# Self-attention's reciprocals two slots behind their maxima, half the transposes and all weighings a slot later, keys projected in other slots

## The chip, the cores and the metric

The kernel runs on one core of a Trainium2 chip. The metric is the device time of one execution in microseconds (us). Three runs of the kernel before took 1098.41, 1099.25 and 1100.58 us; the median is 1099.25. Times inside an execution come from one profiled execution, whose own time was 1095.93 us.

A core has five engines that run their own instruction queues in order: TensorE (PE in the profile; its weight loads are PEld), VectorE (DVE), ScalarE (ACT), GpSimd (POOL) and SyncE (SP), which here issues nearly all transfers. An instruction starts when it has reached the head of its queue and the semaphores that it waits for have come.

## The reference

One transformer block in float32, for 2 sequences of 1024 tokens with 256 features, and a context of 154 tokens with 192 features for each. There are 16 heads of 64, so the attention is 1024 wide. Cut to what matters:

```python
h = layernorm(x, ln1_g, ln1_b)
x = attention(h, h, sa_wq, sa_wk, sa_wv, sa_wo, sa_bo) + x      # self-attention, 1024 keys
h = layernorm(x, ln2_g, ln2_b)
x = attention(h, cond, ca_wq, ca_wk, ca_wv, ca_wo, ca_bo) + x   # cross-attention, 154 keys
h = layernorm(x, ln3_g, ln3_b)
p = h @ ff_w1 + ff_b1
out = (p[..., :1024] * gelu(p[..., 1024:])) @ ff_w2 + ff_b2 + x

def attention(xq, xkv, wq, wk, wv, wo, bo):      # per head, d = 64
    attn = softmax(q @ k.T * 64 ** -0.5)
    return (attn @ v) @ wo + bo
```

## The kernel before, in words

The program is one long sequence written out by hand: a loop over slots p = 0 to 127 for self-attention, one over slots c = 0 to 47 for cross-attention, then the feed-forward part. The order in which the Python code emits instructions is the order in each engine's queue.

**Units and slots.** Heads are taken in pairs; a pair of one sequence is a unit, and there are 16 units. A unit has two halves of 512 queries (index h), and a half has SH = 4 slots. So a unit has 8 slots, and a slot handles 128 queries of two heads, as two groups of 64. In what follows the slots of a half are called 0 to 3.

**A slot of self-attention** (`self_first`, line 642). TensorE makes the scores of the two groups, in two PSUM buffers `s`, 1024 columns each (line 489). Because of the packing of the array, one row of a score tile holds half of a query's 1024 keys for two heads; a query's other half lies 32 partitions away. VectorE takes the maxima of each score tile (line 650). ScalarE makes the exponents into tiles `p` with their sums (`exponents`, line 500; four instructions a slot). SP then sends maxima and sums to the partitions of the other half with four small transfers (`exchange`, line 510; `st<-st` in the profile). In the next slot, `join` (line 514) works out on POOL and ScalarE what the two halves need to share a denominator: differences `dd` (lines 518 and 519), factors `ee` (line 521), products `zz` (line 523) and denominators `den` (line 525). VectorE takes the reciprocal `rd` (line 596) and POOL scales the exponents in place with four instructions (line 600). A slot later still, VectorE transposes the two scaled tiles in blocks of 32 into `pT` (line 614). When the four slots of a half are transposed, TensorE weighs the values with them, in two parts of one slot each (`self_values`, line 618; matmuls at line 535), into two PSUM banks `po`, and ScalarE copies the result out (line 635).

**The order inside slot p before** (loop at line 1139): scores and both maxima of p; copies that the slot before left over; exponents of p; `join` of p-1; the exchange of p; both transposes of p-2 (LAG = 2); an output addition if one is due; the reciprocal and the four scalings of p-1; a bias addition on POOL or a moved transfer if one is due (`later`, in slots 2, 4 and 6 of a unit); weight loads; and last the slot's other work on TensorE. So on VectorE the queue is: maximum, maximum, transpose, transpose (both of p-2), addition, reciprocal (of p-1). On POOL it is: dd, dd, zz, den (of p-1), four scalings (of p-1), bias addition.

**The slot's other work** (lines 1160 to 1178). Slots 2 and 3 of a half weigh the half before. In the first half of a unit, slots 0 and 1 project the next unit's queries and keys (lines 358, 373, 381). In the second half, slot 0 projects the next unit's values (line 389; their second copy goes out by SP, lines 405 and 406), and slot 1 takes two output projections (line 463; VectorE adds them to x, line 470). Layer-norm steps for later use (`norm_beside`, line 322) run beside them: statistics on VectorE (lines 236 and 237), variance and power on POOL (lines 242 and 246), normalisation on ScalarE or POOL, transposition on TensorE (line 276).

**What cross-attention needs from earlier.** The context is transposed (`turn_context`, line 194). Its keys are projected for each of the eight pairs (`context_keys`, line 718; matmuls at line 722; weights by `load_keys`, line 712). Before, pairs 0 to 2 are projected in slot 13, pairs 3 and 4 in slot 125, and pairs 5 to 7 in cross-attention's slot 10. The values of the last 26 context tokens are projected in three pieces (`context_ends`, line 736, 192 columns in each of two halves; EC at line 42).

**Cross-attention** has three slots in a unit: scores, maxima (line 803), exponents (line 814), reciprocal (line 822), scaling (line 825), transposes (line 841), then eight transfers by SP that regroup the transposed tiles (`cross_regroup`, line 847; `wf<-pT_ca` in the profile), and the weighing that reads them (`cross_values`, line 861, `poc` at line 877).

**Buffers.** Tiles `p` come from the pool `pp`, 6 buffers, which at the start also holds the context tiles `cn` and the tile `rows` of layer-norm gains and biases until they are transposed. `pT` has two buffers (one for each of two halves), `s` two, `st8` and the other small tiles four.

Of the kernel before, what the change touches and what calls it, by code (L numbers as in the profile page):

```python
# [8 lines left out]
F32 = mybir.dt.float32  # L9
# [4 lines left out]
P = 128  # L14
# [4 lines left out]
def tile_transformer_block(ctx: ExitStack, tc: tile.TileContext, a: dict, out: bass.AP):  # L19
# [22 lines left out]
    EC = 3 * HR  # L42
# [21 lines left out]
    pp_ = ctx.enter_context(tc.tile_pool(name="pp", bufs=6))  # L64
# [121 lines left out]

    def turn_rows():
        pt = spare["bank"]("p_rows")
        nc.tensor.transpose(
            pt[:, :n_rows - n_cols], rows, ident[:n_rows - n_cols, :n_rows - n_cols]  # L190
        )
        return lambda: nc.scalar.copy(cols[:, n_cols:], pt[:, :n_rows - n_cols])
# [24 lines left out]
    def norm_pieces(kind, b, first=False):  # L217
# [31 lines left out]
        def normalize(t):  # L249
# [5 lines left out]
            pool, tag = (one, "xn") if narrow(kind, b) and not first else (pp_, "P")  # L255

            xn = pool.tile([P, nh, 2, D // nh], F32, tag=tag, name=f"xn_{ln}_{b}_{t}")
            st["xn", t] = xn
# [10 lines left out]
        def turn(t):  # L269
# [4 lines left out]
            for i in range(2 * D // P):  # L274
# [3 lines left out]
                    st["xn", t].rearrange("p c i d -> p (c i d)")[:, i * P:(i + 1) * P], ident)  # L278
# [235 lines left out]
    def join(u, st):  # L514
# [4 lines left out]
        nc.gpsimd.tensor_scalar(dd, dd, 0.0, 1.0, op0=ALU.min, op1=ALU.mult)  # L519
        ee = small.tile([P, 2, 4], F32, tag="ee", name=f"ee_{u}")  # L520
        nc.scalar.activation(ee, dd, AF.Exp)  # L521
        zz = small.tile([P, 2, 4], F32, tag="zz", name=f"zz_{u}")
# [3 lines left out]
        return ee, den  # L526
# [18 lines left out]
    drain = []  # L545
# [42 lines left out]
    joins, groups, halves = [], [], {}  # L588

    def scale_groups(u, st, members):  # L590

        ee, den = join(u, st)

        def reciprocals():
            rd = small.tile([P, 4], F32, tag="rd", name=f"rd_{u}")
            nc.vector.reciprocal(rd, den)  # L596
            for i, pr in enumerate(members):
                for j in range(2):
                    c = 2 * i + j
                    nc.gpsimd.tensor_scalar(  # L600
                        pr[:, j, :], pr[:, j, :], rd[:, c:c + 1], ee[:, 0, c:c + 1],
                        op0=ALU.mult, op1=ALU.mult,
                    )
                groups.append(pr)

        return reciprocals

    def turn_groups(p):
        h, g = divmod(p, SH)
        if g == 0:  # L610
            halves[h] = pt_.tile([P, 2 * NK, QH // 2], F32, tag="pT", name=f"pT_{h}")
        for i in range(2):
            c = (2 * g + i) * KB
            nc.vector.transpose(  # L614
                halves[h][:, :, c:c + KB], groups.pop(0).rearrange("p j (n k) -> p (j n) k", k=KB)
            )
# [25 lines left out]
    def self_first(p):  # L642
# [6 lines left out]
        for i in range(2):  # L649
            nc.vector.tensor_reduce(st[:, 0, 0, i, :], sc[i], AX.X, ALU.max, negate=True)  # L650

        def then():
            members = [exponents(f"{p}_{i}", sc[i], st, i) for i in range(2)]
            late = scale_groups(*joins.pop(0)) if joins else None
            exchange(st)
            joins.append((p, st, members))
            return late
# [25 lines left out]
    def load_ahead(p):  # L683
# [12 lines left out]
        if p == SH:  # L696
            load_keys(0, 3)
        if p == SA - SH - 6:
            load_keys(3, 2)
# [381 lines left out]
    with tc.manual_schedule():  # L1081
# [48 lines left out]
        take("k", 2)  # L1130
        ahead = load_ahead_parts()
        ahead[0] = lambda: load_weights("sa", units[1][1], "k")
        ahead[1] = lambda: load_weights("sa", units[1][1], "q")
        side.append((True, (), turn_rows))
        side.extend((True, (), lambda b=b: turn_context(b)) for b in range(B))
# [3 lines left out]
        for p in range(SA):  # L1139
# [7 lines left out]
            late = then()  # L1147
            if p >= LAG:
                turn_groups(p - LAG)
            if adds:  # L1150
                adds.pop(0)()
            if late:
                late()
# [7 lines left out]
            if h == 0 or hg < LAG:  # L1161

# [3 lines left out]
                ui, n = divmod(p, 2 * SH)  # L1166
                f = (ui - NPAIR // 2 - 1) * EC
                if n == 0 and 0 <= f < DA // 2:
# [167 lines left out]
```

## Time and profile before

| what | value |
|---|---|
| median of three runs | 1099.25 us |
| the profiled execution | 1095.93 us |
| its span, first to last instruction | 1094.1 us |
| self-attention's slots 0 to 127 | 17.9 to about 710 us |
| cross-attention, then feed-forward | to about 871 us, then to the end |

A line of a group in the profile gives the line of the code, the engine, the operation, what it writes and reads, shapes and count; then the busy time of the group and the mean duration of one in ns; then the idle time of the engine just before these instructions, and what ended most of it. A line of a wait names who waited for whom, with the total in us, the number of times and the longest. A line of the timeline gives the start, the duration, the engine, the line of the code, the operation and the number of instructions merged in it; in brackets stands the idle time before it and what ended it. SPq is SyncE's queue of transfers.

### The profile page before, as it was taken

What the parts mean: (1) busy time and instruction counts of PE and PEld (TensorE: products, weight loads), DVE (VectorE), ACT (ScalarE), POOL (GpSimd) and SP (SyncE); (2) the same over time, 40 slices, a digit from 0 to 9 for tenths busy, and PEclk for the clock granted to TensorE, in tenths of its full rate; (3) what the DMA queues carried; (4) which work ended last, traced back from release to release, by engine and by line L of the source; (5) the groups of instructions that cost most, each with busy time, mean ns of one, the idle gap of its engine ahead of it and who ended that gap; (6) DMA issues with size and microseconds to landing.
All of it is one profiled execution on the core that took longest, in us unless ns stands there. A gap on an engine that the chain in (4) does not pass through costs nothing.

```text
span 1094.1 us, 44913 instructions
## 1 busy us (share of the span) xinstructions
PE 1074.5 (98%) x18388; PEld 711.6 (65%) x18388; DVE 892.2 (82%) x1297; ACT 639.2 (58%) x2061; POOL 730.1 (67%) x1552
## 2 busy tenths in 40 slices
PE   8999999999999999999999999899999999999998
PEld 6555666556765565565555655466776677788887
DVE  5889899998989999999999999977877877655442
ACT  5666666667667666666766676565565554242221
POOL 2767777777777777777777777676756785475331
PEclk9999999999999999999999999999999999999999
DMA  3222112122111111111110111036775545000000
GB/s 83 65 59 52 47 44 55 34 51 53 27 40 44 29 43 33 38 42 24 42 42 15 42 30 32 18 82 163 171 172 119 117 108 120 1 10 15 11 15 29
DMA packets 104094, 60.71 MB, mean 55 GB/s; under 512 B 32330, under 2 KB 94674, under 8 KB 103890
## 3 DMA queue, kind: packets, MB, share of 16 engines
q1 hardware_dynamic: 102514, 57.07, 22.1%
q8 instruction: 145, 2.38, 0.9%
q10 hardware_dynamic: 1376, 0.79, 0.3%
q14 instruction: 59, 0.48, 0.1%
HBM read 27.91 MB, written 2.10 MB: 27 GB/s over the span
## 4 chain that ended last, share of the span: by engine, by line
PE 70%; DVE 7%; ACT 7%; DMA 5%; POOL 4%; SPq 3%; issue 3%; DVEq 0%; POOLq 0%; ACTq 0%
PE s L489 13%; PE po L535 12%; ACT p L500 6%; PE pf L1064 5%; PE py_ca L463 5%; PE py_sa L463 4%; DVE st L650 4%; PE pq_ca L358 4%; PE poc L877 4%; DMA st<-st 4%; PE pb L998 3%; PE pv_sa L389 3%; PE sc L798 3%; PE pk_sa L358 3%; SPq L510 3%
## 5 line engine op out<-in xcount | busy, mean ns | idle before, releaser
L500 ACT ACTIVATE p<-s,st 128x512 f32<-128x512 f32 x512 | 345.3, 687 | 196.1 <-DVE st L650 189.8
L600 POOL TENSOR_SCALAR p<-p,rd,ee 128x512 f32<-128x512 f32 x512 | 385.7, 768 | 48.0 <-DVE rd L596 47.0
L650 DVE TENSOR_REDUCE st<-s 128x2 f32<-128x1024 f32 x256 | 300.9, 1216 | 23.4 <-PE s L489 9.1
L614 DVE STREAM_TRANSPOSE pT<-p 128x1024 f32<-128x1024 f32 x256 | 302.3, 1218 | 0.3 <-POOL p L600 0.3
L489 PE MATMUL s<-k_sa,q_sa 64*32 64x512 f32 x4096 | 259.8, 592 | 8.3 <-ACT p L500 7.4
L535 PE MATMUL po<-pT,v_sa 64*32 64x256 f32 x8192 | 239.6, 376 | 0.7 <-DVE pT L614 0.7
L535 PEld LDWEIGHTS po<-pT,v_sa 64*32 64x32 f32 x8192 | 174.2, 106 | 74.8 <-issue 21.2
L489 PEld LDWEIGHTS s<-k_sa,q_sa 64*32 64x32 f32 x4096 | 81.5, 106 | 112.1 <-ACT p L500 56.3
L814 ACT ACTIVATE p<-sc,neg 128x154 f32<-128x154 f32 x256 | 96.4, 406 | 83.7 <-DVE rden L822 80.5
L825 POOL TENSOR_SCALAR p<-p,rden 128x154 f32<-128x154 f32 x256 | 96.8, 398 | 59.1 <-DVE rden L822 58.6
L500 ACT ACTIVATION_READ_ACCUMULATOR p<-s,st 128x1 f32 x512 | 103.9, 203 | 0.0
L523 POOL TENSOR_TENSOR zz<-ee,st 128x8 f32<-128x8 f32 x128 | 25.9, 202 | 74.9 <-ACT ee L521 74.9
L389 PEld LDWEIGHTS pv_sa<-sa_wv,hT_ln 64*128 64x128 f32 x1024 | 58.9, 188 | 14.3 <-issue 5.0
L389 PE MATMUL pv_sa<-sa_wv,hT_ln 64*128 64x128 f32 x1024 | 62.3, 275 | 0.0
L463 PE MATMUL py_ca<-ca_wo,o_ca 128*128 128x256 f32 x256 | 60.0, 382 | 0.5 <-DVE o_ca L891 0.5
L463 PE MATMUL py_sa<-sa_wo,o_sa 128*128 128x256 f32 x256 | 59.7, 385 | 0.0
L518 POOL TENSOR_TENSOR dd<-st 128x8 f32<-128x8 f32 x128 | 25.6, 200 | 50.2 <-DMA st<-st 45.6
L463 PEld LDWEIGHTS py_sa<-sa_wo,o_sa 128*128 128x128 f32 x256 | 47.3, 190 | 17.9 <-ACT v_sa L398 5.9
L358 PE MATMUL pq_sa<-hT_ln,sa_wq 64*32 64x512 f32 (+1 forms) x976 | 58.1, 587 | 0.0
L358 PE MATMUL pq_ca<-hT_ln,ca_wq 64*128 64x512 f32 (+1 forms) x304 | 58.0, 590 | 0.0
L358 PE MATMUL pk_sa<-hT_ln,sa_wk 64*32 64x512 f32 x960 | 57.1, 590 | 0.9 <-ACT q_sa L373 0.9
L803 DVE TENSOR_REDUCE neg<-sc 128x6 f32<-128x924 f32 (+1 forms) x48 | 47.9, 999 | 11.9 <-PE sc L798 11.8
(118 smaller groups left out, 1452.4 us busy)
## 6 DMA issues: line engine op xcount, KB each, us to landing
wf<-pT_ca SPq DMA_DIRECT2D x128, 128.0 KB, 2.4
st<-st SPq DMA_DIRECT2D x512, 1.0 KB, 1.8
v_sa<-v_sa SPq DMA_DIRECT2D x32, 256.0 KB, 3.8
sa_wq<-in_L_xattn_sa_wq_dram SPq DMA_DIRECT2D x32, 128.0 KB, 3.3
sa_wk<-in_L_xattn_sa_wk_dram SPq DMA_DIRECT2D x32, 128.0 KB, 3.0
sa_wv<-in_L_xattn_sa_wv_dram SPq DMA_DIRECT2D x32, 128.0 KB, 3.5
ca_wq<-in_L_xattn_ca_wq_dram SPq DMA_DIRECT2D x32, 128.0 KB, 4.2
wf<-in_L_xattn_ff_w_dram SPq DMA_DIRECT2D x12, 256.0 KB
```

What stands on the lines that cost most here:

```text
L358: nc.tensor.matmul(pq[r][f:f + m, at:at + n], lhsT=wt[own, c, f:f + m], rhs=h[own, c, t0:t0 + n], start=(c == 0), stop=(c == NH - 1), tile ...
L389: nc.tensor.matmul(pv[r][:, i * P:(i + 1) * P], lhsT=h[own, c, i * P:(i + 1) * P], rhs=wt[own, c, :], start=(c == 0), stop=(c == NH - 1), ...
L463: nc.tensor.matmul(py[:, e * D:(e + 1) * D], lhsT=o[:, i, (t + e) * P:(t + e + 1) * P], rhs=wo[kind][:, g * HP + i, :], start=(i == 0), st ...
L489: nc.tensor.matmul(sc[a4 * KB:(a4 + 1) * KB, j, :], lhsT=q[r, c:c + KB], rhs=k[r, h * HB:(h + 1) * HB], start=True, stop=True, tile_positi ...
L500: nc.scalar.activation(pr[:, j, :], sc[:, j, :], AF.Exp, bias=st[:, 0, 0, i, j:j + 1], accum_out=st[:, 0, 1, i, j:j + 1],)
L535: nc.tensor.matmul(po[a2][d:d + KB, :QH // 2], lhsT=v[r, t, e, d:d + KB], rhs=pT[r, d // DH * NK + n, :], start=(t == 0 and e == 0), stop= ...
L600: nc.gpsimd.tensor_scalar(pr[:, j, :], pr[:, j, :], rd[:, c:c + 1], ee[:, 0, c:c + 1], op0=ALU.mult, op1=ALU.mult,)
L614: nc.vector.transpose(halves[h][:, :, c:c + KB], groups.pop(0).rearrange("p j (n k) -> p (j n) k", k=KB))
L650: nc.vector.tensor_reduce(st[:, 0, 0, i, :], sc[i], AX.X, ALU.max, negate=True)
L814: nc.scalar.activation(pr_[:, j, i, :T], sc[:, j, i * T:(i + 1) * T], AF.Exp, bias=neg[:, j, i:i + 1], accum_out=den[:, j, i:i + 1],)
L825: nc.gpsimd.tensor_scalar(pr_[:, j, i, :T], pr_[:, j, i, :T], rden[:, j, i:i + 1], 1.0, op0=ALU.mult, op1=ALU.mult,)
L1064: nc.tensor.matmul(own[:, :D], lhsT=ub[pair][j][:, f, e * P:(e + 1) * P], rhs=w2[:, f, :], start=(f == 0), stop=(f == NF - 1),)
```

## The change

- **Reciprocals and scaling.** The reciprocal of slot p-2 stands between the two maxima of slot p, where before the reciprocal of p-1 stood behind the transposes. The four scalings of p-2 run in slot p: two ahead of `dd` of p-1, one behind it, one behind `den` of p-1.
- **Transposes.** In slot p VectorE transposes the second tile of p-3 and then the first tile of p-2, where before it transposed both tiles of p-2. The pool of `p` tiles gets a seventh buffer.
- **Weighing.** A half is weighed in slot 3 of the next half and slot 0 of the one after, so queries and keys move to slots 1 and 2 of a unit, values to slot 5 and output projections to slot 6. The first half's slots shift accordingly: slot 6 has no weighing. The last two halves are weighed in slot 127 and cross slot 0, and in cross slots 3 and 4 as before.
- **Keys.** Context keys are projected two pairs at a time: pairs 0 and 1 in slots 1 and 2 (one each), then two pairs in slots 6, 14 and 126. None is left in cross slot 10. Both context tiles are transposed in slot 0, and the tile `rows` in slot 3. The ends go in four pieces of 128 columns instead of three, loaded and projected later in their units.
- **Normalised tiles.** For layer norms of self-attention and of the first sequence's cross-attention, the normalised tile before transposition is written to the place in `hT` that the transposed one takes over, instead of to a buffer of its own.

The diff, cut to its core:

```diff
-    EC = 3 * HR
+    EC = P
-    pp_ = ctx.enter_context(tc.tile_pool(name="pp", bufs=6))
+    pp_ = ctx.enter_context(tc.tile_pool(name="pp", bufs=7))
...
+            if narrow(kind, b) and not first:
+                xn = st["hT"][:, :, t * P // 2:(t + 2) * P // 2].rearrange(
+                    "p c (i d) -> p c i d", i=2)
...
-    def scale_groups(u, st, members):
...
+    def reciprocals(p):
+        if p < 0:
+            return
+        own = slots[p]
+        own["rd"] = small.tile([P, 4], F32, tag="rd", name=f"rd_{p}")
+        nc.vector.reciprocal(own["rd"], own["den"])
+
+    def scale_rows(p, c0, c1):
+        if p < 0:
+            return
+        own = slots[p]
+        for c in range(c0, c1):
+            i, j = divmod(c, 2)
+            pr = own["p"][i]
+            nc.gpsimd.tensor_scalar(
+                pr[:, j, :], pr[:, j, :], own["rd"][:, c:c + 1], own["ee"][:, 0, c:c + 1],
+                op0=ALU.mult, op1=ALU.mult,
+            )
+
+    def join(p):
+        scale_rows(p - 1, 0, 2)
+        if p >= 0:
+            own = slots[p]
+            dd = differences(p, own["st"])
+            own["ee"] = factors(p, dd)
+        scale_rows(p - 1, 2, 3)
+        if p >= 0:
+            own["den"] = denominators(p, own["st"], own["ee"])
+        scale_rows(p - 1, 3, 4)
...
         for i in range(2):
             nc.vector.tensor_reduce(st[:, 0, 0, i, :], sc[i], AX.X, ALU.max, negate=True)
+            if i == 0:
+                reciprocals(p - 2)
 
         def then():
-            members = [exponents(f"{p}_{i}", sc[i], st, i) for i in range(2)]
-            late = scale_groups(*joins.pop(0)) if joins else None
+            slots[p] = {"st": st, "p": [exponents(f"{p}_{i}", sc[i], st, i) for i in range(2)]}
+            join(p - 1)
             exchange(st)
...
-        if p == SH:
-            load_keys(0, 3)
-        if p == SA - SH - 6:
-            load_keys(3, 2)
+        if p in (LAG + 1, 2 * SH - 1, SA - SH - 6):
+            load_keys(2 * (1 + (LAG + 1, 2 * SH - 1, SA - SH - 6).index(p)), 2)
...
-            late = then()
-            if p >= LAG:
-                turn_groups(p - LAG)
+            then()
+            turn_group(p - LAG - 1, 1)
+            turn_group(p - LAG, 0)
             if adds:
                 adds.pop(0)()
-            if late:
-                late()
...
-            if h == 0 or hg < LAG:
+            if h and hg == SH - 1:
+                run(lambda: self_values(h - 1, 0))
+            elif h > 1 and hg == 0:
+                run(lambda: self_values(h - 2, 1))
+            else:
                 run_work(2 if p < SA - SH else 1, h % 2 or h == 0, sum_tile)
...
-                if n == SH + 1 and ui in (1, NU - 1):
-                    pr = 0 if ui == 1 else 3
+                if n == SH + LAG and ui in (0, 1, NU - 1):
+                    pr = {0: 2, 1: 4, NU - 1: 6}[ui]
                     run(lambda: context_keys(pr, sum_tile))
-                    kept.extend(context_keys(pr + i, mm_tile) for i in range(1, 3 if ui == 1 else 2))
-            else:
-                run(lambda: self_values(h - 1, hg - LAG))
+                    kept.append(context_keys(pr + 1, mm_tile))
...
-            if c == 2 * len(CG):
-                load_keys(5, 3)
...
-            if c == 2 * SH + 2:
-                for pr, bank in ((5, sum_tile), (6, sum_tile), (7, mm_tile)):
-                    run(lambda: context_keys(pr, bank))
```

## The prediction

> **What bounds the kernel now.** I read the page first (busy shares, the granted clock, the costliest groups), then the waits, then the timeline engine by engine, slot by slot, in self-attention, and last the timeline around the key projections of cross-attention.
>
> ```profile
> PE 1074.5 (98%) x18388; PEld 711.6 (65%) x18388; DVE 892.2 (82%) x1297; ACT 639.2 (58%) x2061; POOL 730.1 (67%) x1552
> PEclk9999999999999999999999999999999999999999
> L500 ACT ACTIVATE p<-s,st 128x512 f32<-128x512 f32 x512 | 345.3, 687 | 196.1 <-DVE st L650 189.8
> L600 POOL TENSOR_SCALAR p<-p,rd,ee 128x512 f32<-128x512 f32 x512 | 385.7, 768 | 48.0 <-DVE rd L596 47.0
> L650 DVE TENSOR_REDUCE st<-s 128x2 f32<-128x1024 f32 x256 | 300.9, 1216 | 23.4 <-PE s L489 9.1
> L614 DVE STREAM_TRANSPOSE pT<-p 128x1024 f32<-128x1024 f32 x256 | 302.3, 1218 | 0.3 <-POOL p L600 0.3
> ```
>
> TensorE is nearly always busy at an unthrottled clock, but VectorE is close behind it in self-attention (span 17.9 to 710 us): each of the 128 slots holds two maxima and two transposes of 1.22 us and one reciprocal of 0.18. Started back to back they follow each other at 1.14, so VectorE's shortest round is about 4.8 us. The waits:
>
> ```profile
> POOL dd L518 <- DMA st<-st: 45.6, 38, 13.5
> DVE rd L596 <- POOL den L525: 30.9, 43, 3.0
> ```
>
> Now two pairs of neighbouring slots from TensorE's timeline (start, duration; a slot runs from its first score matmul to the next slot's):
>
> ```profile
> 319.28 1.92 PE L489 MATMUL s<-k_sa,q_sa 64*32 64x512 f32 x32
> 321.00 3.66 PE L535 MATMUL po<-pT,v_sa 64*32 64x256 f32 x128
> 324.45 1.92 PE L489 MATMUL s<-k_sa,q_sa 64*32 64x512 f32 x32
> ...
> 60.06 1.92 PE L489 MATMUL s<-k_sa,q_sa 64*32 64x512 f32 x32
> 61.78 3.64 PE L358 MATMUL pq_sa<-hT_ln,sa_wq 64*32 64x512 f32 x64
> 66.54 1.09 PE L489 MATMUL s<-k_sa,q_sa 64*32 64x512 f32 x16 [1.12 <-ACT p L500]
> ```
>
> The first slot (55) takes 324.45 - 319.28 = 5.17, scores plus weighing with nothing between. The second (8) takes 6.48: TensorE waits for exponents. What made them late stands in the timelines of SP, POOL and DVE:
>
> ```profile
> 56.74 4.13 SPq L510 DMA_DIRECT2D st<-st  x4
> ...
> 62.09 0.20 POOL L518 TENSOR_TENSOR dd<-st 128x8 f32<-128x8 f32 x1 [2.79 <-DMA st<-st]
> ...
> 58.58 2.36 DVE L614 STREAM_TRANSPOSE pT<-p 128x1024 f32<-128x1024 f32 x2
> 63.47 0.18 DVE L596 RECIPROCAL rd<-den 128x4 f32<-128x4 f32 x1 [2.53 <-POOL den L525]
> 63.77 2.36 DVE L650 TENSOR_REDUCE st<-s 128x2 f32<-128x1024 f32 x2
> ```
>
> A late exchange (56.74, behind the value moves) makes the denominator late; the reciprocal waits 2.53 at the head of VectorE's queue; the maxima behind it start at 63.77 though their scores were done at 61.3; so exponents, so the next scores. In all slots from 4 on I took this table: length, and where the first maximum starts (R) after the first score. On time R is +1.25. Undisturbed lengths are 5.15 to 5.17 (query, key, weighing), 5.62 (values; 6.21 with a turned tile), 5.53 (output). R up to about +2.0 costs nothing (slot 33: +1.96, length 5.15); beyond that the slot grows. Excess over the undisturbed length where R is +2.0 or more, slot: us: 5: 0.38, 8: 1.32, 9: 0.51, 12: 0.12, 14: 0.24, 15: 0.36, 17: 1.16, 36: 0.47, 39: 0.49, 40: 0.72, 41: 0.51, 79: 0.36, 81: 0.27, 86: 0.11, 87: 0.49, 89: 0.23, 99: 0.28, 100: 0.33, 105: 0.30. Sum 8.65; other slots up to 123 add some 2.5 that has no late maximum.
>
> **The change part by part.** Durations are those of the profiled execution (1095.93 us, span 1094.11), which is 3.3 below the median of the runs (1099.25); I add the differences to the median.
>
> Part 1, reciprocals and scaling. No instruction is added or removed; the order changes. Before, the denominator of slot p-1 is ready at R+4.7 (exponents end R+3.95, ee +0.28, zz and den 0.57) and needed at R+4.7, after the transposes: no slack, hence 43 waits. Then even on-time rounds show about 0.11 idle before the reciprocal and 0.12 behind it, a round of 5.04. After, its reciprocal stands behind the first maximum of slot p+1, at R+5.17+1.14 = R+6.3, while den is ready at about R+5.0 (one scaling of 0.75 now stands ahead of zz, but inside POOL's wait for ee). Slack 1.3. Of the waits for den only five in the timeline reach 1.3 (3.05, 2.53, 1.71, 1.44, 1.31); for the one quoted, dd at R+5.8 gives den at about R+7.5 and a wait of 0.2 instead of 2.53. A shorter round (4.8 against TensorE's 5.15) also works off the output additions (two of 0.65 a unit) and statistics (two of 0.58) faster: 8 x 4.8 + 2.9 = 41.3 a unit, under TensorE's 42.1.
> New waits: POOL's first two scalings wait for the reciprocal (R+1.5 to R+3.0); behind them stand dd (then ee on ScalarE) and the rest. The exchange lands at about R+2.7, so dd loses nothing; ee is ready at R+3.6, exponents end at R+3.95, so ScalarE and the query, key and value copies behind ee lose nothing. The first transpose of p-2 needs the pair at R+3.3; VectorE reaches it at R+3.6. What covers this is POOL's idle time: its last scaling ends 0.5 into the next round, 1.0 before the reciprocal. A bias addition (0.73) fits; variance and power (0.19 + 0.71) beside one do not, which makes about 0.35 in 8 slots, within the 0.75 by which R may slip free. Without that cover each 0.1 us in every slot costs 12.8. The reciprocal between the maxima delays the second exponents by at most 0.15, against 0.5 that TensorE leaves them.
> So of the 8.65 I take 90%: -7.8. Bounds: -3 (VectorE stays late from its own extra work: only the five long waits' slots, 7/8/9 and 16/17, recover) and -11.2 (all excess).
> A port rule speaks against this part. All 512 scalings took 760 to 780 ns, beside maxima and transposes alike, so I charge nothing. The Trainium skill (SBUF — State Buffer, section on the two separate sides) says VectorE and GpSimd share a port pair under an exclusive lock, held for a whole instruction when VectorE runs a two-port mode or reads two SBUF inputs. If the transposes took it, the second scaling of a pair would wait for one; as an estimate by that page the round would then close at 5.8, and the sum would be a loss of some 80 us.
>
> Part 2, the later transpose and weighing. Everything on TensorE from slot 6 on keeps its order but moves one slot; seven buffers replace six, and slots wait for none of them except slot 3 (there the row tile is still held, so its second exponents wait for a transpose, as slot 2's did before). End pieces against end pieces: before, slots 13 (three keys) 5.33, 124 4.63, 125 5.31, 126 5.67, 127 5.12, and 2.64 to the query projection at 712.76: 28.70. After, four short slots (6, 14, 125, 126), one weighing slot 5.17, and cross slot 0 with a weighing: 0.9 + 3.45 + 0.9 = 5.3. A short slot is VectorE's: 4.9, between 4.8 and the 5.31 of slot 125. 19.6 + 5.17 + 5.3 = 30.1: +1.4, less 0.72 that the last half's weighing waited for its transpose at 721.85, where two projections now stand between: +0.65 (bounds +0.2 and +2.3).
>
> Part 3, keys. Each key product costs TensorE 1.2 (three: 3.69).
>
> ```profile
> 752.70 3.75 PE L722 MATMUL pk<-ctxT,ca_wk 96*128 96x320 f32 x12
> 756.39 1.09 PE L877 MATMUL poc<-wf,v_ca 64*64 64x256 f32 x16
> ...
> 747.48 6.44 SPq L858 DMA_DIRECT2D wf<-pT_ca  x8
> ```
>
> Three leave cross slot 10, where TensorE has no gap: up to -3.7. But the weighing behind them reads what SP's eight regroupings bring; the eighth is issued at 753.33 and such a one lands 2.4 later, 755.8. The weighing's second half, which would start at 752.70 + 1.4 = 754.1, waits to about 756.0: -3.69 + 1.9 = -1.8 (bounds -0.8, if c12's scores then wait for slot 10's exponents, and -3.7).
> Two go to slots 1 and 2. Scores of slot 2 then start near 27.5 (26.68 before), but its maxima started at 28.83, behind a reciprocal's 3.05 wait that is gone; followed through, slot 3's second scores come near 33.4 (34.23), slot 3's buffer wait gives 0.4 back, slot 5 starts near 43.5 (43.70): -0.2 (bounds -1.5, +1.2).
> On SP: key loads (0.45 each to issue) become four, at the start and in slots 3, 7 and 118; SP issues 2.47 of exchange and up to 1.36 of weights in a 5.15 slot, so they fit. Ends in four pieces of 128 columns: 4 x 0.57 (slot 61 against 5.53) for 0.79 + 0.79 + 0.57: +0.1; two more DMAs, under the same cover. Normalised tiles in hT's own place: same instructions, 0.
>
> Sum: -7.8 + 0.65 - 1.8 - 0.2 + 0.1 = -9.1: the profiled execution 1086.9, the runs 1090.2.
>
> **The rivals.** (a) VectorE stays late by its own load, not by den: for it, slots 12 to 15 and 76 to 79 (rounds 5.54 and 5.2, den waits only 0.1); against it, those rounds lose 0.22 of wait each. Then -3 + 0.65 - 0.8 - 0.2 + 0.1 = -3.2: 1096.
> (b) Slower: the loop inside a slot, maximum 1.14, reciprocal 0.1, 0.29, pair 1.51, 0.3, transpose 1.14, closes at 4.5 of 5.17. It decides once the pair is 0.7 late in most slots. At 0.8: 128 x 0.1 = 12.8, with none of the 7.8: 1099.25 + 12.8 - 1.25 = 1110.8. For it: POOL is busy 3.9 a slot; against: nothing but biases and norms is added, in 24 slots.
> (c) Everything recovers: -11.2, -3.7, -1.5 and +0.3: 1083.
> (d) The reciprocal still waits for den, because den now stands behind a scaling. The gain on waits vanishes and only keys remain: 1098. It takes den 1.3 later than I have it.
>
> **How the numbers follow.** Forecast (-6 to -12) 0.60, (a) 0.15, (b) 0.10, (c) 0.10, (d) 0.05. This kernel's measurement tells apart about 0.2%, 2.2 us. Slower is (b); same is (d) and a little of (a); the rest is faster: 0.84, 0.06, 0.10. The range leaves out (b), part of (c) and part of (d): 1084 to 1098.
>
> **What would show it.** Right: den waits before the reciprocal under 6 us in total; R mostly at +1.25 and no later than +2; weighing slots 5.17 nearly everywhere; no key products after slot 127, and a wait for the regrouping in cross slot 10. Wrong: VectorE's transposes waiting for POOL's scalings by more than 10 us, ee late on ScalarE with key or output projections waiting for copies, or short slots over 5.3.

## The result and the profile after

The changed kernel took 1086.05 us (median of four runs, 1085.40 to 1086.37) beside 1098.83 for the kernel before on the same chip: a ratio of 0.9881, 95% interval 0.9864 to 0.9898. The forecast was 1090.2, range 1084 to 1098. By the ratio the gain is 13.1 us, 11.2 to 14.9. The profiled execution of after took 1086.05 as well, 9.9 less than the profiled one of before; the sum had said 9.1 less. That the medians differ by 12.8 comes from before's profiled execution, which was some 3 us faster than its median.

The page of after: busy shares, clock, and the four groups that were shown of before.

```profile
PE 1069.9 (99%) x18404; PEld 705.2 (65%) x18404; DVE 879.8 (81%) x1297; ACT 644.3 (59%) x2062; POOL 730.5 (67%) x1552
PEclk9999999999999999999999999999999999999999
L619 POOL TENSOR_SCALAR p<-p,rd,ee 128x512 f32<-128x512 f32 x512 | 392.6, 772 | 82.6 <-DVE rd L609 80.9
L508 ACT ACTIVATE p<-s,st 128x512 f32<-128x512 f32 x512 | 345.5, 687 | 164.1 <-DVE st L681 152.1
L681 DVE TENSOR_REDUCE st<-s 128x2 f32<-128x1024 f32 x256 | 308.5, 1206 | 55.4 <-issue 18.4
L644 DVE STREAM_TRANSPOSE pT<-p 128x1024 f32<-128x1024 f32 x256 | 303.0, 1219 | 3.4 <-POOL p L619 3.3
```

The instructions take what they took (scalings 772 ns against 768, transposes 1219 against 1218, maxima 1206 against 1216). What changed is the idle time ahead of them: VectorE is idle longer ahead of maxima (55.4 against 23.4), exponents wait less for maxima (152.1 against 189.8), and scalings wait for the reciprocal (80.9 against 47.0), which costs nothing, since the transposes behind them wait 3.3 in all. The waits that were shown of before:

```profile
POOL dd L526 <- DMA st<-st: 78.6, 67, 14.5
DVE rd L609 <- POOL den L539: 5.5, 7, 2.3
```

The reciprocal waits 5.5 in all, where it waited 30.9; the differences wait more than before (78.6 against 45.6), at no cost that shows here. A round of VectorE (from one slot's first maximum to the next slot's) in an undisturbed slot, and the work of GpSimd for it (two timelines; x2 merges two instructions):

```profile
323.05 1.21 DVE L681 TENSOR_REDUCE st<-s 128x2 f32<-128x1024 f32 x1
324.18 0.15 DVE L609 RECIPROCAL rd<-den 128x4 f32<-128x4 f32 x1
324.25 1.19 DVE L681 TENSOR_REDUCE st<-s 128x2 f32<-128x1024 f32 x1
325.36 2.36 DVE L644 STREAM_TRANSPOSE pT<-p 128x1024 f32<-128x1024 f32 x2
328.16 1.23 DVE L681 TENSOR_REDUCE st<-s 128x2 f32<-128x1024 f32 x1 [0.44 <-ACT q_sa L381]
```
```profile
322.67 0.20 POOL L539 TENSOR_TENSOR den<-zz 128x4 f32<-128x4 f32 x1
322.84 0.77 POOL L619 TENSOR_SCALAR p<-p,rd,ee 128x512 f32<-128x512 f32 x1
324.43 1.52 POOL L619 TENSOR_SCALAR p<-p,rd,ee 128x512 f32<-128x512 f32 x2 [0.81 <-DVE rd L609]
```

The denominator ends at 322.87 and its reciprocal starts at 324.18, 1.31 later. The pair of scalings starts 0.10 behind the reciprocal's end and ends at 325.95, 0.55 before VectorE comes to the transpose that needs it (325.36 + 1.14 = 326.50). VectorE then has 0.44 left before the next scores.

The exchange that came late in before (slot 6's, needed in slots 7 and 8) is late here too, though less, and this is what it does now:

```profile
54.93 4.04 SPq L518 DMA_DIRECT2D st<-st  x4
...
60.19 0.20 POOL L526 TENSOR_TENSOR dd<-st 128x8 f32<-128x8 f32 x1 [1.79 <-DMA st<-st]
...
61.96 0.18 DVE L609 RECIPROCAL rd<-den 128x4 f32<-128x4 f32 x1 [0.25 <-POOL den L539]
...
59.26 1.93 PE L497 MATMUL s<-k_sa,q_sa 64*32 64x512 f32 x32
...
64.42 0.63 PE L497 MATMUL s<-k_sa,q_sa 64*32 64x512 f32 x6
```

The differences start at 60.19 after a wait of 1.79 (62.09 and 2.79 before); the reciprocal waits 0.25 where it waited 2.53, and the slot takes 5.17 (59.26 to 64.42, where the next scores begin) instead of 6.48. Not all of that is the reciprocal's new place: the differences come 0.93 behind the start of slot 8 here and 2.03 in before, so about half of the 2.28 is an exchange that is 1.1 less late (the transfers are issued 0.15 behind the last exponent, 54.78, and 1.52 behind it in before, 55.22).

Where the time went, from the starts of the same work in the two timelines of TensorE: at the start 0 (slot 5 begins at 43.71 against 43.70); by slot 120, -10.0, of which -1.5 is two short slots (6 and 14, 4.23 each with 0.29 more in the slot behind, where before's slot 13 took 5.33 and one more weighing slot 5.17); from slot 120 to cross slot 1, +1.8; in cross slot 10, -2.07; at the end of the span -9.85. Short pieces and end section together stand at +0.7 by the prediction's own list: 29.44 against its 28.70.

### The profile page after: what moved, and what is told of

It reads as the page before. It is cut to its first block, busy times and chain, and to the rows that moved or that the text cites. A ratio compares the mean times of both kernels' runs of the same rounds, so it can differ in the third digit from the quotient of the medians.

```text
span 1084.3 us, 44882 instructions
## 1 busy us (share of the span) xinstructions
PE 1069.9 (99%) x18404; PEld 705.2 (65%) x18404; DVE 879.8 (81%) x1297; ACT 644.3 (59%) x2062; POOL 730.5 (67%) x1552
## 4 chain that ended last, share of the span: by engine, by line
PE 89%; DVE 3%; POOL 2%; DMA 2%; SPq 1%; ACT 1%; issue 1%; POOLq 0%; ACTq 0%; DVEq 0%
PE po L549 19%; PE s L497 19%; PE py_sa L471 5%; PE pf L1093 5%; PE py_ca L471 5%; PE pv_sa L397 5%; PE pk_sa L366 5%; PE pq_sa L366 4%; PE poc L906 4%; PE pq_ca L366 4%; PE pb L1027 4%; PE sc L827 3%; PE pa L1027 2%; PE pc L1027 2%; DMA st<-st 2%; SPq L518 1%
## 5 line engine op out<-in xcount | busy, mean ns | idle before, releaser
L619 POOL TENSOR_SCALAR p<-p,rd,ee 128x512 f32<-128x512 f32 x512 | 392.6, 772 | 82.6 <-DVE rd L609 80.9
L508 ACT ACTIVATE p<-s,st 128x512 f32<-128x512 f32 x512 | 345.5, 687 | 164.1 <-DVE st L681 152.1
L681 DVE TENSOR_REDUCE st<-s 128x2 f32<-128x1024 f32 x256 | 308.5, 1206 | 55.4 <-issue 18.4
L644 DVE STREAM_TRANSPOSE pT<-p 128x1024 f32<-128x1024 f32 x256 | 303.0, 1219 | 3.4 <-POOL p L619 3.3
L497 PE MATMUL s<-k_sa,q_sa 64*32 64x512 f32 x4096 | 251.4, 591 | 2.5 <-ACT p L508 1.8
L549 PE MATMUL po<-pT,v_sa 64*32 64x256 f32 x8192 | 236.4, 376 | 0.9 <-DVE pT L644 0.9
L549 PEld LDWEIGHTS po<-pT,v_sa 64*32 64x32 f32 x8192 | 170.4, 106 | 78.1 <-issue 29.9
L497 PEld LDWEIGHTS s<-k_sa,q_sa 64*32 64x32 f32 x4096 | 78.9, 106 | 102.9 <-issue 52.9
L526 POOL TENSOR_TENSOR dd<-st 128x8 f32<-128x8 f32 x128 | 25.9, 202 | 80.9 <-DMA st<-st 78.6
L843 ACT ACTIVATION_READ_ACCUMULATOR p<-sc,neg 128x1 f32 x256 | 56.9, 222 | 0.0
```

The source lines that it names most:

```text
L497: nc.tensor.matmul(sc[a4 * KB:(a4 + 1) * KB, j, :], lhsT=q[r, c:c + KB], rhs=k[r, h * HB:(h + 1) * HB], start=True, stop=True, tile_positi ...
L508: nc.scalar.activation(pr[:, j, :], sc[:, j, :], AF.Exp, bias=st[:, 0, 0, i, j:j + 1], accum_out=st[:, 0, 1, i, j:j + 1],)
L549: nc.tensor.matmul(po[a2][d:d + KB, :QH // 2], lhsT=v[r, t, e, d:d + KB], rhs=pT[r, d // DH * NK + n, :], start=(t == 0 and e == 0), stop= ...
L619: nc.gpsimd.tensor_scalar(pr[:, j, :], pr[:, j, :], own["rd"][:, c:c + 1], own["ee"][:, 0, c:c + 1], op0=ALU.mult, op1=ALU.mult,)
L644: nc.vector.transpose(halves[h][:, :, c:c + KB], slots[p]["p"][i].rearrange("p j (n k) -> p (j n) k", k=KB))
L843: nc.scalar.activation(pr_[:, j, i, :T], sc[:, j, i * T:(i + 1) * T], AF.Exp, bias=neg[:, j, i:i + 1], accum_out=den[:, j, i:i + 1],)
```

## The experiments

Times are given against the kernel before on the same chip. Where a run is set against the changed kernel, the two ratios are subtracted (0.0010 is 1.1 us) and their intervals are added as squares.

**1. The first part alone undone.** The reciprocal of p-1 goes back behind the transposes, and the scalings with it; everything else stays changed.

```diff
-        scale_rows(p - 1, 0, 2)
...
-        scale_rows(p - 1, 2, 3)
...
-        scale_rows(p - 1, 3, 4)
...
-            if i == 0:
-                reciprocals(p - 2)
...
             if adds:
                 adds.pop(0)()
+            reciprocals(p - 1)
+            scale_rows(p - 1, 0, 4)
             flush(kept)
```

> The changed kernel with its first part alone undone: the reciprocal of slot p-1 stands again behind slot p's transposes and additions, and its four scalings behind the denominators; the later transposes and weighings, the seventh buffer and the keys stay as changed. Theory (slack of the denominator): the waits of the reciprocal come back to about 31 us in 40 to 45 places, late first maxima come back, and the time is 8 to 10 above the changed kernel's 1086.1, so 1094 to 1096, some 3 to 5 below the kernel before. Rival (the later transposes or weighings do it, not the reciprocal's place): at most 1 us above the changed kernel, 1086 to 1087. Rival (VectorE late by its own load): 3 above, 1089.

Measured: 1099.17 us, ratio 1.0004 (0.9986 to 1.0022): 13.5 ± 2.7 above the changed kernel, and all of the gain is gone.

```profile
DVE rd L609 <- POOL den L539: 39.9, 62, 3.6
...
391.29 1.92 PE L497 MATMUL s<-k_sa,q_sa 64*32 64x512 f32 x32
394.33 0.18 DVE L609 RECIPROCAL rd<-den 128x4 f32<-128x4 f32 x1 [2.30 <-POOL den L539]
394.64 2.35 DVE L677 TENSOR_REDUCE st<-s 128x2 f32<-128x1024 f32 x2
...
690.45 1.92 PE L497 MATMUL s<-k_sa,q_sa 64*32 64x512 f32 x32
```

The waits for denominators are back, and the first maxima again start as late as R = +3.35 (slot 69, the three lines from 391.29). Slot 124 begins at 690.45 against 679.00 of after:

```profile
679.00 1.92 PE L497 MATMUL s<-k_sa,q_sa 64*32 64x512 f32 x32
```

So the place of the reciprocal with its scalings, and neither the later transposes nor VectorE's own load, carries the gain in self-attention. The size is above what was expected (8 to 10). The later transposes, weighings and keys together are worth 0 ± 2 without it.

**2. The reciprocal one place later.** It stands behind both maxima (`i == 1` for `i == 0`), so that the denominator has still more slack and the loop inside a slot is longer.

```diff
-            if i == 0:
+            if i == 1:
                 reciprocals(p - 2)
```

> The changed kernel with the reciprocal of p-2 one place later, behind both maxima instead of between them. Nothing else is moved, and the denominator's slack grows by 1.14. Theory with the loop inside a slot (maximum, reciprocal, pair of scalings, first transpose): the reciprocal starts at R+2.3 instead of R+1.15, the pair ends at R+4.25, VectorE reaches the first transpose of p-2 at R+3.6 and waits for it to about R+4.5, so its round is 5.7 against the 5.15 of a slot: 0.55 in each of some 110 slots, +60 us, about 1146, with transposes waiting for scalings by 0.9 a slot. Rival (only the denominator's slack counts, POOL has time to spare): no change, 1086.

Measured: 1112.26 us, ratio 1.0123 (1.0106 to 1.0140), 26.6 ± 2.6 above the changed kernel. The loop exists, but it is cheaper than I had it. VectorE and GpSimd in a slot of that run:

```profile
DVE pT L644 <- POOL p L619: 68.0, 127, 1.7
```
```profile
338.12 2.31 DVE L681 TENSOR_REDUCE st<-s 128x2 f32<-128x1024 f32 x2
340.36 0.16 DVE L609 RECIPROCAL rd<-den 128x4 f32<-128x4 f32 x1
340.44 1.21 DVE L644 STREAM_TRANSPOSE pT<-p 128x1024 f32<-128x1024 f32 x1
342.16 1.25 DVE L644 STREAM_TRANSPOSE pT<-p 128x1024 f32<-128x1024 f32 x1 [0.52 <-POOL p L619]
343.35 2.36 DVE L681 TENSOR_REDUCE st<-s 128x2 f32<-128x1024 f32 x2
```
```profile
340.61 1.52 POOL L619 TENSOR_SCALAR p<-p,rd,ee 128x512 f32<-128x512 f32 x2 [1.25 <-DVE rd L609]
```

The reciprocal ends at 340.52; the pair starts at 340.61 and ends at 342.13; the transpose starts at 342.16. The two hand-overs (from the end of one engine's instruction to the start of the other's that waited for it) take 0.09 and 0.03; I had priced them at 0.29 and 0.3. The round is 5.23 (343.35 - 338.12), not 5.7, and exceeds a slot of 5.15 by 0.08, or by 0.66 where an output addition joins (the next instruction starts 0.58 behind its start). A unit takes 44.2 (325.18 to 369.40) against 42.8 of after (316.62 to 359.40): 1.4 in 16 units is 23 us.

**3. One more scaling, inside and outside the pair.** The extra instruction scales a row by 1.0: same size, same engine. It took 0.62, where 0.75 was expected.

```diff
             pr = own["p"][i]
+            if c == 0:        # the other kernel: c == 3
+                nc.gpsimd.tensor_scalar(
+                    pr[:, j, :], pr[:, j, :], 1.0, 1.0, op0=ALU.mult, op1=ALU.mult)
             nc.gpsimd.tensor_scalar(
```

> The changed kernel with one more scaling (by 1.0, same size, 0.75 us on GpSimd) ahead of the first scaling of every slot, inside the pair that the first transpose of p-2 waits for. With the loop as the prediction priced it (closes at 4.5 of 5.17): 5.25, so about +10 us. With the loop as the run with the reciprocal behind both maxima shows it (the pair starts 0.10 behind the reciprocal and the transpose 0.02 behind the pair, against 0.29 and 0.3 as priced): the pair ends at R+3.65, VectorE reaches that transpose at R+3.46, waits 0.2, and the round is 4.9 of 5.15: 0 to +4 us, transposes waiting for scalings by 15 to 30 us in all.

> The changed kernel with the same extra scaling, but behind the third one, ahead of the fourth and last of each slot, outside the pair. Theory (GpSimd waits 0.2 to 1.1 for the reciprocal each round): the pair starts up to 0.5 late in some slots and the transpose waits less than with the extra one inside the pair: 0 to +2 us. Rival (GpSimd's sum, 4.65 of 5.15, is what counts, not the place): the same time as with the extra scaling inside the pair, within 1 us.

Measured: 1087.49 (ratio 0.9908, 0.9889 to 0.9927) and 1088.46 (0.9922, 0.9907 to 0.9936): 3.0 ± 2.8 and 4.5 ± 2.5 above the changed kernel; by the profiled executions 1.3 and 2.4.

```profile
PE 1069.9 (99%) x18404; PEld 710.9 (65%) x18404; DVE 880.9 (81%) x1297; ACT 644.1 (59%) x2062; POOL 801.2 (74%) x1680
DVE pT L647 <- POOL p L622: 11.7, 21, 1.2
```

This is the page and a wait of the first of the two. GpSimd does 71 us more and the kernel loses some 3 of them: it has that cover. With the hand-overs as the second experiment shows them, the loop closes at 4.1 instead of 4.5 (1.13 + 0.15 + 0.10 + 1.52 + 0.03 + 1.14), and at 4.7 with the extra scaling, still under a slot of 5.15. The second kernel's transposes waited as much (12.3), so the place of the extra instruction made no difference that these runs resolve, and my reason for expecting one, that the tail is free, has no support. The expected 15 to 30 us of waits were 11.7.

**4. A later exchange, in both kernels.** Two of the four transfers are split in two, so that six are issued; then one of the four, so that five are.

```diff
-            nc.sync.dma_start(
-                out=st[a4 * KB:(a4 + 1) * KB, 1], in_=st[o4 * KB:(o4 + 1) * KB, 0]
-            )
+            for k in ((slice(0, 1), slice(1, 2)) if a4 < 2 else (slice(0, 2),)):   # five: a4 < 1
+                nc.sync.dma_start(
+                    out=st[a4 * KB:(a4 + 1) * KB, 1, k], in_=st[o4 * KB:(o4 + 1) * KB, 0, k]
+                )
```

> The kernel before with two of the four transfers of each exchange split in two (maxima and sums apart), so that its last transfer is issued some 1.24 us later in every slot of self-attention. Theory (no slack ahead of the reciprocal): the denominator follows, some 0.6 of the 1.24 being hidden where the factors wait for ScalarE anyway; the reciprocal waits in nearly every slot, VectorE's round grows from 5.04 to some 5.6, and each of about 116 slots by 0.45: +50 us, bounds +20 and +100. Rival (the exchange is not what sets the reciprocal): under +5.

> The changed kernel with the same split of the exchange. Theory (1.3 to 1.5 of slack between denominator and reciprocal): 0 to +4 us above the changed kernel's 1086.1, the waits for denominators stay under 15 us in all. Rival (the gain was the order of the work, and a later exchange costs as much here): +50 as in the kernel before. Rival (SyncE's queue, 3.71 of exchange beside 1.36 of weights in a 5.15 slot, becomes full): weights land late and the time rises by 10 or more with TensorE waiting for weights.

> The kernel before with one of the four transfers of each exchange split in two (maxima and sums apart): its last transfer is issued some 0.62 us later, and SyncE's queue has five transfers a slot instead of four or six. Theory (no slack ahead of the reciprocal; some 0.35 of it hidden where the factors wait for ScalarE): the round of VectorE grows from 5.04 to some 5.3, over the 5.15 of a slot: +15 to +30 us. Rival (it was the full queue that made six transfers dear, not the reciprocal): under +5.

> The changed kernel with the same five transfers. With six it lost 42 us although the denominators were in time in most slots: its factors (ee, on ScalarE) came late and the copies queued behind them kept TensorE waiting, 20 of the 42 in slots 2 and 6 of a unit, which follow weight loads and value moves on SyncE's queue. Theory (slack of the denominator plus a queue that five transfers, 3.1 to 3.9 us a slot beside weights, do not fill): 0 to +6 us. Rival (ScalarE's wait for the factors has no slack at all): about half of the 42 that six cost, +20.

Measured: from the kernel before, 1157.52 us with six (ratio 1.0561, 1.0537 to 1.0585: 62 us more) and 1103.77 with five (1.0059, 1.0037 to 1.0081: 6.5 more); from the changed kernel, 1128.34 with six (1.0289, 1.0270 to 1.0307: 45 ± 3 above the changed kernel) and 1092.45 with five (0.9954, 0.9936 to 0.9972: 8 ± 3 above it). The +50 for before with six came near; before with five was far under the +15 to +30, and nearer to the under +5 of its rival, a full queue; after with six, where I had expected almost nothing, was a plain miss (its waits for denominators, expected under 15, were 38.2), and after with five lies at the edge of its 0 to 6. The rival of a full queue named 10 or more for after with six, but by way of late weights, and TensorE waits for something else:

```profile
POOL dd L527 <- DMA st<-st: 162.4, 99, 15.0
ACT ee L533 <- POOL dd L528: 125.1, 94, 5.3
DVE rd L610 <- POOL den L540: 38.2, 41, 4.4
PEld pk_sa L366 <- ACT q_sa L381: 23.4, 27, 2.0
PEld py_sa L471 <- ACT v_sa L406: 17.8, 12, 2.4
```

These are waits of the changed kernel with six. In the kernel before with six, the reciprocal waits twice as long:

```profile
DVE rd L597 <- POOL den L526: 84.7, 87, 3.7
```

A late exchange has two ways to TensorE. One goes through the denominator and the reciprocal at the head of VectorE's queue; the change gave that one slack. The other goes through the factors `ee` on ScalarE, in front of the copies of queries, keys and values; by the prediction's own times ScalarE comes to `ee` 0.35 after it could run (R+3.95 and R+3.6), and the change gave nothing there: the wait of `ee` is 125.1 (38.9 in after), and TensorE waits for what stands behind it: weight loads for keys 23.4 (3.7 in after), for outputs 17.8 (5.4), for scores, which need the exponents, 48.2 (19.5). In the middle slot the slack holds: the median round of VectorE over slots 20 to 117 of the timelines goes from 5.17 to 5.20 in after and from 5.33 to 5.63 in before. In after it is a part of the slots that pays: slots 2 and 6 of the units, which project keys and outputs, hold 22.7 of the 41.0 us by which slots 0 to 126 lengthen. The round that one in ten exceeds goes from 6.1 to 6.6 in after and from 5.9 to 6.7 in before. Nor is the delay what I set. With six, the differences start 0.9 (before) or 1.1 (after) later behind the last exponent in the median; with five, 0.0 or 0.1, and 0.2 to 0.4 at the level that one slot in ten exceeds. The chain that ended last shows where the six went: SyncE's queue, 20% of it where after has 1% (and 18% in the kernel before with six).

```profile
SPq L519 20%; DMA st<-st 11%; PE pf L1094 5%; PE py_ca L471 5%; ACT p L508 4%; PE po L550 4%; PE poc L907 4%; PE pb L1028 3%; PE pq_ca L366 3%; PE s L497 3%; POOL p L620 3%; PE sc L828 3%; PE py_sa L471 3%; PE pa L1028 2%; PE pc L1028 2%
```

So these runs mix a later exchange with a fuller queue, and how much of the 45 is due to each stays open. What they do show is that the slack is for the reciprocal, and that late exchanges still cost where they reach ScalarE. The changed kernel stays ahead throughout: by 29 us with six transfers, 11 with five and 13 with four.

**5. The three keys left out of cross slot 10, in the kernel before.** Their keys are copies of three others, made in slot 13.

```diff
...
-            if c == 2 * len(CG):
-                load_keys(5, 3)
...
-                for pr, bank in ((5, sum_tile), (6, sum_tile), (7, mm_tile)):
-                    run(lambda: context_keys(pr, bank))
```

> The kernel before with the three key products left out of cross-attention's slot 10 and nothing put elsewhere: the keys of pairs 5 to 7 are copies of those of pairs 0 to 2, made by three more copies in slot 13, so the result is another. Theory (the weighing behind them waits for the regrouping): 1.8 to 2.1 below the kernel before, with TensorE waiting some 1.6 to 1.9 ahead of or inside the weighing that followed the keys. Rival (the products were on the path with all their time): 3.7 below. Rival (hidden anyway): 0.

Measured: 1096.56 us, ratio 0.9979 (0.9965 to 0.9994): -2.3, between -0.7 and -3.8. The timeline of TensorE, whose work stands within 0.02 us of before's ahead of this place, gives the amount better: cross slot 11 begins at 757.40 against 759.14, so -1.74. By the end of the span 0.9 of it is left (1093.2 against 1094.1).

```profile
752.72 1.10 PE L882 MATMUL poc<-wf,v_ca 64*64 64x256 f32 x16
753.63 0.61 PE L882 MATMUL poc<-pT_ca,v_ca 64*64 64x256 f32 x8
755.12 0.65 PE L882 MATMUL poc<-wf,v_ca 64*64 64x256 f32 x4 [0.87 <-ACT q_ca L373]
755.96 0.87 PE L882 MATMUL poc<-wf,v_ca 64*64 64x256 f32 x10 [0.19 <-DMA wf<-pT_ca]
...
757.40 0.80 PE L803 MATMUL sc<-kT,q_ca 64*128 64x154 f32 x8
```

And cross slot 11 of the kernel before:

```profile
759.14 0.79 PE L798 MATMUL sc<-kT,q_ca 64*128 64x154 f32 x8
```

The second half of the weighing waits 0.87 and then 0.19. The first and longer wait ends with ScalarE's copy of the queries, which the theory had not seen. But the wait that ends last, at 755.96, is for the regrouping, as the theory had it: in order, all but four of the half's matmuls would have stood until then without the copy, too.

**6. Two further moves at the ends, tried for a faster kernel.** The reciprocal of slot 127 goes behind the transposes of 126, and the value moves of unit 2 behind the regrouping.

```diff
-            if c < 2:
-                reciprocals(SA - 2 + c)
+            if c == 0:
+                reciprocals(SA - 2)
...
                 turn_group(SA - 2, 1)
+                reciprocals(SA - 1)
...
-            for _ in range(min(2, len(later))):
+            for _ in range(min(2 if c != SH + 3 else 0, len(later))):
```

> The changed kernel with two more moves in cross-attention. (1) In cross slot 1 the reciprocal of self-attention's slot 127 stands behind the transposes of 126 instead of ahead of them: it waited 2.34 for its denominator with ready transposes behind it, and the weighing of the last half waited 0.91 for the transposes of 127. Expected -0.9. (2) The six moves of the values of unit 2 are issued one cross slot later, so behind the eight regroupings that cross slot 10's weighing reads, which then can start at 737.6 to 739.0 instead of 739.44 and end some 1.9 earlier. Expected -0.6 (the wait alone) to -1.5. Sum -1.5 to -2.4: 1083.7 to 1084.6. Rival (the waits reappear one step later, at the scaling of 127 and at the first half's readers): 0.

Measured: 1086.41 us, ratio 0.9901 (0.9883 to 0.9919), so 2.2 ± 2.7 above the changed kernel: no gain.

```profile
708.66 1.25 DVE L644 STREAM_TRANSPOSE pT<-p 128x1024 f32<-128x1024 f32 x1 [1.31 <-POOL p L619]
709.83 0.14 DVE L609 RECIPROCAL rd<-den 128x4 f32<-128x4 f32 x1
```
```profile
714.41 3.69 PE L549 MATMUL po<-pT,v_sa 64*32 64x256 f32 x128 [1.20 <-DVE pT L644]
...
747.67 1.35 PE L906 MATMUL poc<-wf,v_ca 64*64 64x256 f32 x14 [0.88 <-ACT q_ca L381]
```
```profile
737.91 6.07 SPq L887 DMA_DIRECT2D wf<-pT_ca  x8
```
```profile
746.99 1.11 ACT L381 ACTIVATE q_ca<-pq_ca 128x512 f32<-128x512 f32 x2
```

The first move made a new wait of the kind that the change had removed: the second transpose of 126 was not ready, and the reciprocal behind it came at 709.83 instead of 708.24; the last half's weighing waited 1.20 instead of 0.91. The second move did bring the regrouping forward (issued from 737.91 to 744.02, where after's ran from 739.44 to 745.74), and the weighing's second half still came 2.41 behind the first (2.43 in after). It starts as the first of the two copies of queries ends on ScalarE (746.99 and half of 1.11), and that copy stands behind six exponents. So here the copy ends the wait, and the regrouping, 1.5 earlier than in after, is not what holds it.

**7. Six buffers for the exponents instead of seven.**

```diff
-    pp_ = ctx.enter_context(tc.tile_pool(name="pp", bufs=7))
+    pp_ = ctx.enter_context(tc.tile_pool(name="pp", bufs=6))
```

> The changed kernel with six buffers for the exponents instead of seven, and nothing else. The second exponents of slot p then take the place of the second tile of p-3, which is transposed in slot p itself, behind both maxima: they start at R+3.5 instead of R+2.3, ScalarE ends 1.2 later, at R+5.1, the exchange leaves 1.2 later and the next scores wait about 0.7 for their buffer. Theory: +0.7 in each of some 110 slots, +75 us, with ScalarE's second exponents waiting for transposes. Rival (the transposed tile comes free early enough): 0 to +5.

Measured: 1117.54 us, ratio 1.0188 (1.0161 to 1.0215), 33.7 ± 3.5 above the changed kernel. The exponents wait for the transposes as expected:

```profile
ACT p L508 <- DVE pT L644: 133.0, 126, 2.8
```

They end at R+5.02 (median), but a slot grows by 0.23 on average and not by 0.7: with R at +1.25 they end at 6.3 in the slot, and the next slot's second scores want their buffer at 5.17 + 0.95 = 6.1. In the prediction I allowed TensorE 0.5 there; it has 0.9. The seventh buffer is a condition of the change: without it the kernel is slower than before.

**8. The normalised tiles' place alone, in the kernel before.**

```diff
-            pool, tag = (one, "xn") if narrow(kind, b) and not first else (pp_, "P")
+            if narrow(kind, b) and not first:
+                xn = st["hT"][:, :, t * P // 2:(t + 2) * P // 2].rearrange(
+                    "p c (i d) -> p c i d", i=2)
...
```

> The kernel before with the normalised tiles of layer norm written to their later place in hT instead of to a buffer of their own, and nothing else. Theory: no difference, within 0.5 us. Rival (writes into hT wait for the readers of the tile before, or free the normalisation of its buffer): 1 us or more either way.

Measured: 1099.99 us, ratio 1.0011 (0.9998 to 1.0024). No difference can be told; 0.5 us is finer than these runs resolve, and the interval, -0.2 to +2.6, does not exclude the rival's 1 us on the slower side.

## Why the prediction was right, point by point

- **The size.** Profiled execution against profiled execution the sum was close, -9.9 for -9.1. By the medians it was -12.8, outside the -6 to -12 that was given 0.60, and 1086.05 lies nearer to rival (c)'s 1083 than to 1090.2. The closeness of the first pair is in part luck: the execution of before that was profiled was 3 us faster than the median.
- **Part 1, -7.8.** Right in mechanism, and undersized. Of the excess of some 11.2 that the slot table of before holds, the same table of after keeps some 2.3 (most of it in slots 5, 10, 13, 70), so some 8.9 went, and the starts of slot 124 say the same (10.4 earlier, of which 1.5 is the two short slots). That is more than the 7.8 taken as 90% of the 8.65 in slots with a late maximum: that list leaves out slots 35, 92 and 108 (R of 2.1 to 2.6, some 0.5 in all), and some of the other excess seems to be of the same cause. The denominator's slack, 1.3 by the prediction, is 1.31 in the slot shown and 1.48 in the median of slots 20 to 117. With it, the wait of 2.53 in slot 8 would have become 1.2 (2.53 - 1.3), not the 0.2 that the prediction names; the 0.25 that was measured goes with an exchange 1.1 less late. Nor do two additions of 0.65 and two statistics of 0.58 make 2.9 a unit, but 2.5; nothing hangs on it, since VectorE stays under TensorE either way. Undoing the part alone costs 13.5 ± 2.7 by the runs. That is above the 8.9 of the table; that the profiled execution of before held less of these waits than most of its runs would explain it, but no second execution of before was profiled.
- **New waits on GpSimd, 0.** Right: transposes wait 3.3 in all. The hand-overs were overpriced at 0.29 and 0.3 (0.09 to 0.10 and 0.03), so the loop has a margin of 1.1 rather than 0.7, and rival (b) was less near than its chance of 0.10 said. Experiments 2 and 3 show the loop and the margin.
- **The port rule.** Had the transposes taken the exclusive lock of which the Trainium skill tells (SBUF — State Buffer, section on the two separate sides), a scaling would have stood behind a transpose. In the round shown, the pair's second scaling runs beside the first of the two transposes, and the pair takes 1.52; no run here shows the lock for these instructions.
- **Part 2, +0.65.** The sum was nearly right (+0.9), by luck, from two misses that offset each other. The short pieces cost +0.7 instead of +1.4 (short slots of 4.23, 4.23, 4.00 and 5.09, not 4.9). The wait of 0.72 ahead of the last half's weighing did not vanish: it is 0.91, because the reciprocal of 127 waits 2.34 for its denominator in cross slot 1, and VectorE, from its start at 708.24, works without a gap through what stands behind it to the end of the transposes of 127 at 713.77. The step that failed is "two projections now stand between": the transposes moved back as far as the weighing did.
- **Part 3, -1.8.** The amount was right at its place: -1.74 with the products alone left out, -2.07 in the changed kernel. The reason was incomplete. I had the weighing's second half wait for the eighth regrouping to about 756.0. With the products alone left out it does, to 755.96, but it stands first for ScalarE's copy of the queries, behind six exponents (0.87 of 1.06); in the changed kernel that copy alone ends the wait (experiment 6). So the sign "a wait for the regrouping in cross slot 10" did not come.
- **Start, -0.2; ends, +0.1; tiles' place, 0.** Slot 5 begins at the same time to 0.01, so the start gave nothing. The ends were not tried alone.
- **The other signs.** The reciprocal waits 5.5 for denominators, under the 6 named. R is under +1.45 in 109 of the slots 4 to 123 and passes +2 in one of them (slot 15, +2.33). No short slot takes more than 5.09.
- **Rivals.** (a) falls with experiment 1, where VectorE's load is that of after and the whole gain goes. (b) falls with the result. (c) is too large by 3, and by the medians nearer than the forecast. (d) falls with the 5.5 of waits.

## What to carry to other kernels

When an instruction on a nearly full engine waits at the head of its queue for a result that came through other engines and a transfer, use the result one round later: the engine then works through what is ready, at the price of one more buffer and a later consumer. Before doing so, follow the loop that the move creates inside a round (here maximum, reciprocal, scalings, transpose), since a move of one place made the difference between 13 us gained and 13 us lost. And list every queue that a late transfer reaches: slack given to one (VectorE's) was not seen to help another (ScalarE's).

## What the runs showed of the hardware that I had not expected

- The scatter between runs went with the waits. The kernel before lay between 1094.39 and 1103.01 in 29 runs, and the one with the reciprocal put back between 1095.50 and 1106.54 in 12; the changed kernel lay within 1.0 us in four runs, and the one of experiment 6, which has the same self-attention, within 1.2 in six. But the first kernel of experiment 3, whose waits for denominators are as short (5.1), spread over 3.2 in four runs, and four runs of before over 2.7. That slack absorbs transfers that land at different times is a reading that fits most of this; it was not tried by itself.
- A fifth transfer in an exchange (one of the four of 1 KB sent as two of 0.5 KB) put the differences at most 0.1 later in the median, where I had expected the 0.62 of one more issue. With six, 0.9 to 1.1 of the expected 1.24 came.
- From the end of an instruction on VectorE to the start of the one on GpSimd that waited for it, 0.09 to 0.10 went by in experiment 2, and 0.03 on the way back.
